# State sums for two tiles at a time, convolution taps loaded per image, and two edits at the first scan, in a four-layer convolutional block

## The chip, the cores and the metric

The kernel runs on one core of a Trainium2 chip. A core has five engines, each with its own instruction queue: TensorE (PE; matmuls, with its weight loads listed as PEld), VectorE (DVE), ScalarE (ACT), GpSimd (POOL) and SyncE (SP), which here issues nearly all DMA transfers. Within an engine instructions run in order; between engines they wait for one another by semaphores. Matmuls write to PSUM, which has eight banks of 128 x 512 float32; everything else lives in SBUF, 128 partitions wide, or in DRAM. The metric is the device time of one execution in microseconds.

## What is computed

The input x is 4 images of 128 channels and 64 x 64 pixels in float32. Four layers follow, each of the form x + layer(group norm of x), with 32 groups. Cut to what matters:

```python
# layer 0: attention over the 4096 pixels of an image (q, k, v from 128x128 matrices)
x = x + attention(gn(x))
# layer 1: 5x5 convolution whose 25 taps are built from radial tables
x = x + conv5(gn(x), build_kernel(weightsxx, weightsidentity, ...))
# layer 2: state space layer, channels 0-63 forward and 64-127 backward in the pixels
t  = Wx @ gn(x)
xc = silu(causal_conv4(t))                     # per direction, 64 channels
delta = softplus(Wd @ xc);  B = WB @ xc;  C = WC @ xc
h[l] = exp(delta * A) * h[l-1] + delta * xc * B   # 64 states per channel
y  = sum_over_states(h * C) + D * xc
x = x + Wp @ y
# layer 3: 3x3 convolution (its offset branch does not change the result)
x = x + conv3(gn(x), main_w) + main_b
```

For one image and one direction the state is 64 channels x 64 states, and the recurrence runs over 4096 pixels.

## The kernel before

**The scan and its ticks.** The recurrence of layer 2 is done by `scan_core` (L1160) as 1024 ticks of 128 rows x 1024 pixels. The ticks of an image (256 of them) run over four chunks of pixels, two directions d, 16 groups q of four states, and two halves g of 32 channels: a tile's 128 rows are 32 channels x 4 states. A tick i consists of steps that are issued at different distances, so that engines overlap: `load` four ticks ahead (SP fetches delta and delta*x, `de` and `dx`, spread over the states, when q is 0, and the B and C rows, `br` and `cr`, spread over the channels, when g is 0), `drive` two ahead (GpSimd, db = dx * br, L1228), `decay` one ahead (ScalarE, two exponentials of 512 pixels into PSUM banks, L1221), `recur` (VectorE, the scan itself, L1238, and for three ticks in five the product with C, L1241), `weigh` one behind (GpSimd, the product with C for the others, L1259) and `collect` three behind (TensorE). `collect` (L1261) does nothing for g = 0. For g = 1 it multiplies the two finished state tiles hc with a 128 x 32 selection matrix `sel` that sums over four states: four matmuls, one for each combination of half chunk and channel half, each into its own 32 partitions of one bank y (L1273). The bank gathers all 16 groups q; then the skip term D * xc is added (L1284), ScalarE copies the bank out, and SP stores it. State tiles hc come from a pool of six buffers (L1500).

**Work beside the scan.** All else is one long Python generator, `images` (L1450), and the main loop (L1518) draws from it. Each piece of work says what it costs TensorE in estimated microseconds; per tick 2.8 of such units are drawn (1.5 in the last image). So the order of instructions of every engine is fixed when the program is built. While image b is scanned, image b+1 goes through its front: its load and norm (`start`, `attention_start`), attention, the 5x5 convolution (`conv_pairs`) and the operands of its own scan (`scan_operands`). While image 3 is scanned, the ends of images 0 to 2 are done: output projection and 3x3 convolution. Image 0's own front runs alone at the beginning, and image 3's end alone at the end.

**Attention** (L434) walks through 256 steps u per image: a block of scores of 128 x 512 (L479), its exponential by ScalarE into a ring of eight 512-wide slots (L485), and the product with v two steps later (L491). The ring lies in a tile named `exchange`, which later holds delta. For image 0 the softmax sums are gathered by VectorE and GpSimd; for the others every four steps a group of four 32-column matmuls (`sums`, L507, tile zp) adds four ring slots. `sums_due` holds such a group back for up to a few steps, until a `collect` has just been issued (the flag "collected").

**The 5x5 convolution** works on pairs of rows. Its weights are the 25 taps, the sums of two pairs of tap rows (SUM12, SUM34), and for image 0 two further combinations (`more`). `build_conv_weights` (L231) makes taps and sums once, during image 0's attention, in a constant tile `cw` of 35 matrices of 128 x 128; `more_weights` makes the combinations in a pool `fill` that lives only until image 0's convolution is done. The first 15 matrices of `cw` are overwritten for the last layer (`m3`, LSUM, LDIF) when the last convolution is done, so they are also stored to DRAM (`kept`), from where a second, safe run of the program would get them back. That second run is taken only where softmax sums leave a range.

**Operands of the scan** (`scan_operands`, L998): per 512 pixels tap products (tile pt, `taps`), half of them into xc and their tanh (`halves`, L1030), the silu from both (`silu`, L1043), three products of xc (delta, B, C), softplus in several ScalarE steps, and stores to DRAM, from where the scan's rows are fetched. For image 0 the tanh goes to an SBUF buffer of the pool tag "w" (four buffers, shared with the B and C rows on their way out); for the others it stays in the bank pt.

**The load of image 1** (`start`, L1358, called beside image 0's operands with after = 10): it waits until image 0's operands no longer read the buffer (the flag "read"), lets ten turns pass, loads four pieces of 512 KB, lets ten more pass, and then takes the norm's statistics.

Of the kernel before, what the change touches and what calls it, by code (L numbers as in the profile page):

```python
# [24 lines left out]
F32 = mybir.dt.float32  # L25
# [7 lines left out]
P = 128  # L33
# [19 lines left out]
def conv_preact_kernel(  # L53
# [166 lines left out]


    SUM12, SUM34, HSUM, HDIF = 5, 6, 7, 8
    cw = const.tile([P, NTAP + 10, C], F32, name="cw")
    taps5 = cw[:, :NTAP, :]

    m3 = cw[:, : main_w.shape[1], :]

    LSUM, LDIF, NKEPT = 9, 12, 15
    kept = dram.tile([P, NKEPT, C], F32, tag="kept", bufs=1, name="kept")

    def build_conv_weights(tmp):  # L231
        xx_sb = tmp.tile([P, NTAP, C], F32, name="xx_sb")
        nc.sync.dma_start(xx_sb, xhat)
        id_sb = tmp.tile([P, C], F32, name="id_sb")
        nc.sync.dma_start(id_sb, identity)
        picked = tmp.tile([P, 2, NTAP, C // 2], F32, name="picked")
        for n, (which, table, inds) in enumerate((("xx", wxx, indsxx), ("id", wid, indsid))):
            nr, oc = table.shape[1], table.shape[2]
            acc = picked[:, n]
            one = cw.rearrange("p k c -> p (k c)")[:, : NTAP * oc]  # L240
            one = one.rearrange("p (k o) -> p k o", o=oc)
            tab = tmp.tile([P, nr, oc], F32, name=f"tab{which}")
            nc.sync.dma_start(tab, table)
            ii = tmp.tile([P, NTAP], I32, name=f"ii{which}")
            nc.sync.dma_start(ii, inds.to_broadcast([P, NTAP]))
            fi = tmp.tile([P, NTAP], F32, name=f"fi{which}")
            nc.vector.tensor_copy(fi, ii)

            ng = tmp.tile([P, NTAP], F32, name=f"ng{which}")
            nc.vector.tensor_scalar(ng, fi, 0.0, float(nr), ALU.is_lt, ALU.mult)  # L250
            nc.vector.tensor_tensor(fi, fi, ng, ALU.add)
            nc.vector.tensor_scalar(fi, fi, 0.0, float(nr - 1), ALU.max, ALU.min)
            for r in range(nr):
                hit = tmp.tile([P, NTAP], F32, name=f"hit{which}{r}")
                nc.vector.tensor_scalar(hit, fi, float(r), None, ALU.is_equal)
                hit_b = hit.unsqueeze(2).to_broadcast([P, NTAP, oc])
                tab_b = tab[:, r : r + 1, :].to_broadcast([P, NTAP, oc])
                if r == 0:
                    nc.vector.tensor_tensor(acc, tab_b, hit_b, ALU.mult)
                else:  # L260
                    nc.vector.tensor_tensor(one, tab_b, hit_b, ALU.mult)
                    nc.vector.tensor_tensor(acc, acc, one, ALU.add)
                yield HOP

        for t in range(2):
            def every(ap):
                return ap.rearrange("p k (o t) -> p k o t", t=2)[:, :NTAP, :, t]

            idb = id_sb.rearrange("p (o t) -> p o t", t=2)[:, :, t].unsqueeze(1)
            idb = idb.to_broadcast([P, NTAP, C // 2])  # L270
            nc.vector.tensor_tensor(every(xx_sb), every(xx_sb), picked[:, 0], ALU.mult)
            nc.vector.tensor_tensor(every(cw), picked[:, 1], idb, ALU.mult)
            yield HOP
        nc.vector.tensor_tensor(taps5, taps5, xx_sb, ALU.add)
        for n in range(2):
            row = cw[:, (1 + 2 * n) * 5 :]
            nc.vector.tensor_tensor(
                cw[:, NTAP + n * 5 : NTAP + (n + 1) * 5, :], row[:, :5], row[:, 5:10], ALU.add
            )
        nc.sync.dma_start(kept, cw[:, :NKEPT, :])  # L280

# [152 lines left out]
    def attention(b, xs, xn, v, st, safe, loads):  # L434
# [264 lines left out]


    def last_weights():
        half, above = cw[:, LSUM : LSUM + 3, :], cw[:, LDIF : LDIF + 3, :]
        nc.vector.tensor_tensor(half, m3[:, 0:3, :], m3[:, 6:9, :], ALU.add)
        nc.vector.tensor_scalar(half, half, 0.5, None, ALU.mult)
        nc.vector.scalar_tensor_tensor(above, m3[:, 3:6, :], -0.5, half, ALU.mult, ALU.add)
        nc.vector.scalar_tensor_tensor(half, m3[:, 3:6, :], 0.5, half, ALU.mult, ALU.add)

    def conv_last(b, xs, st, finish):
# [8 lines left out]
        def flat(t):  # L717
            return t.rearrange("p (h w) -> p h w", w=W)
# [30 lines left out]
        def products(acc, view, w):  # L749

            for n, dx in enumerate((1, 0, 2)):
                to = slice(max(1 - dx, 0), W - max(dx - 1, 0))
                of_ = slice(max(dx - 1, 0), W - max(1 - dx, 0))
                nc.tensor.matmul(  # L754
                    flat(acc)[:, :, to], cw[:, w + dx, :], view[:, :, of_],
                    start=n == 0, stop=n == 2, skip_group_check=True,
                )

# [36 lines left out]

    def more_weights(to):
# [12 lines left out]
    def conv_pairs(b, xs, tag, st, st2, lean):  # L811
# [99 lines left out]
        for c in range(L // CH):  # L911
# [20 lines left out]
            for n, (acc, parts) in enumerate(accs):  # L932
                k, total = 0, len(parts) * K5
                for w, view, r in parts:
                    for dx in range(K5):
                        k += 1
                        nc.tensor.matmul(  # L937
                            flat(acc), cw[:, w * K5 + dx, :] if w < HSUM else more[:, w - HSUM, dx, :],
                            view(r, dx), start=k == 1, stop=k == total and (n == 0 or not lean),
                        )  # L940
# [57 lines left out]
    def scan_operands(b, xn, mats4, piece):  # L998
# [31 lines left out]
        def halves(i):  # L1030
# [129 lines left out]
    def scan_core(mats4, ynds, before, widen, result):  # L1160
# [100 lines left out]
        def collect(i):  # L1261
# [2 lines left out]
            b, c, d, q, g = ticks[i]  # L1264
            if g + 1 < KG:
                return
            if q == 0:
                yacc[0] = bank("y", f"y_{b}_{c}_{d}")
            y = yacc[0]
            for h in range(CH // MM):  # L1270
                for gg in range(KG):
                    r = h * HALF + gg * SG
                    nc.tensor.matmul(  # L1273
                        y[r : r + SG, :], sel, hcs[i - KG + 1 + gg][:, bass.ts(h, MM)],
                        start=q == 0, stop=False, tile_position=(0, r), skip_group_check=True,
                    )
            ready.add("collected")
            for gg in range(KG):
                del hcs[i - KG + 1 + gg]
            if q + 1 < NQ:  # L1280
                return
            for h in range(CH // MM):
# [62 lines left out]
    def program(safe):  # L1345
# [2 lines left out]
        ready.clear()  # L1348
        shared.clear()
        if safe:  # L1350
            nc.sync.dma_start(cw[:, :NKEPT, :], kept)

        def load(tile, b):
            for c in range(NCH):
# [109 lines left out]
        with ExitStack() as es, tc.manual_schedule():  # L1464
# [19 lines left out]
            if not safe:  # L1484
                with tc.tile_pool(name="fill", bufs=2) as pools["fill"]:
                    while not (0, "begun") in ready:
                        next(work)
                    more = pools["fill"].tile([P, 2, 5, C], F32, tag="more", bufs=1, name="more")

                    with tc.tile_pool(name="tables", bufs=1) as tmp:  # L1490
                        for _ in chain(scan_constants(), build_conv_weights(tmp), more_weights(more)):
# [117 lines left out]
```

## Time and profile before

| what | value |
|---|---|
| median of three runs | 4463.48 us (4461.15 to 4466.09) |
| profiled run, and the span of its profile | 4455.06 us, 4453.2 us |
| TensorE busy in the span | 3977.4 us, 89% |
| VectorE busy | 3725.2 us, 84% |
| GpSimd busy | 3638.9 us, 82% |
| ScalarE busy | 2399.5 us, 54% |
| first and last drive (db) of scan 0 | 682 and 1635 us |
| of scan 1 | 1640 and 2583 us |
| of scan 2 | 2586 and 3529 us |
| of scan 3 | 3537 and 4375 us |
| scores of images 0, 1, 2, 3 | from 28, 731, 1676, 2620 us |

The span is the time from the first to the last instruction of the profiled execution; what lies around it makes the difference of 2 us to that run's time. A busy share over the whole span mixes stages with different limits. It must be read by stage, for which the drives give the borders: one tick has one drive, 256 ticks are a scan. The groups of the page that bear on the change (line, engine, operation, out<-in, count; then busy time, mean ns of one, and idle time before it with what ended most of it):

```profile
L1273 PE MATMUL y<-hc,sel 128*32 128x512 f32 x4096 | 652.1, 650 | 272.9 <-POOL hc L1259 264.6
L513 PE MATMUL zp<-exchange,ones 128*32 128x512 f32 x1536 | 201.6, 596 | 7.9 <-DVE xs L580 7.9
L1228 POOL TENSOR_TENSOR db<-dx,br 128x1024 f32<-128x1024 f32 x1024 | 2400.1, 2366 | 223.0 <-DMA dx<-dxd 53.1
```

A float32 matmul appears as two passes, so 4096 stands for 2048 matmuls in 512 calls of `collect`. Four of them run side by side in the array, hence 652 us busy at 650 ns each. The 265 us in which TensorE waits for a state tile lie almost wholly in scan 3, where TensorE has little to do.

### The profile page before, as it was taken

The page shows a single profiled execution, that of the slowest core. Times are in us where ns is not written, and L with a number is a line of the kernel's source. Part 1 is how long each engine was busy: PE and PEld are TensorE (multiplying, and loading weights), DVE is VectorE, ACT ScalarE, POOL GpSimd, SP SyncE. Part 2 cuts the span into 40 slices and gives each one's busy share as a digit, 9 for nine tenths or more (in the row PEclk, how much of TensorE's full clock was granted, in tenths as well). Part 3 has the DMA queues.
Part 4 walks back from the last instruction along what each step waited for, and adds up shares of the span by engine and source line. Part 5 has one row for each costly group of instructions (what it writes and reads, how often), then busy time and mean ns, then how long its engine had stood idle before and what let it go on. Part 6 is the DMA issues. An engine that isn't in the chain of part 4 may idle for free. (4 is left out here: it accounts for less than half of the span.)

```text
span 4453.2 us, 43584 instructions
## 1 busy us (share of the span) xinstructions
PE 3977.4 (89%) x13480; PEld 1470.5 (33%) x13480; DVE 3725.2 (84%) x3703; ACT 2399.5 (54%) x4425; POOL 3638.9 (82%) x1728
## 2 busy tenths in 40 slices
PE   8999998999999979999999989999999658576776
PEld 4444433333333323333333333333333112121222
DVE  4721218999999989999999899999999899999995
ACT  3333226666665476666664576666654754444532
POOL 3433307999999978999999889999999889999995
PEclk9999999999999989999999989999999878787888
DMA  1000016545554565454545565454545656656562
GB/s 63 9 1 1 0 59 229 177 169 175 177 175 157 178 231 196 173 174 172 182 158 175 200 227 175 172 181 170 177 160 177 224 213 210 226 197 231 188 227 79
DMA packets 210002, 719.86 MB, mean 162 GB/s; under 512 B 24800, under 2 KB 25696, under 8 KB 209632
## 3 DMA queue, kind: packets, MB, share of 16 engines
q1 hardware_dynamic: 208160, 716.26, 45.9%
q8 instruction: 108, 1.77, 0.2%
q14 instruction: 134, 1.10, 0.1%
q10 hardware_dynamic: 1600, 0.73, 0.1%
HBM read 649.07 MB, written 67.83 MB: 161 GB/s over the span
## 5 line engine op out<-in xcount | busy, mean ns | idle before, releaser
L1228 POOL TENSOR_TENSOR db<-dx,br 128x1024 f32<-128x1024 f32 x1024 | 2400.1, 2366 | 223.0 <-DMA dx<-dxd 53.1
L1221 ACT ACTIVATE da<-de,a_neg 128x512 f32<-128x512 f32 (+1 forms) x1796 | 1343.4, 751 | 683.3 <-DVE da L1238 393.7
L479 PE MATMUL sc<-r,x 128*128 128x512 f32 x2048 | 1085.2, 612 | 4.3 <-ACT r L448 3.2
L491 PE MATMUL acc<-exchange,v 128*128 128x512 f32 x2048 | 1047.7, 593 | 1.6
L1259 POOL TENSOR_TENSOR hc<-hc,cr 128x1024 f32<-128x1024 f32 x401 | 948.3, 2365 | 19.0 <-ACT last L1254 15.6
L485 ACT ACTIVATE exchange<-sc 128x512 f32<-128x512 f32 x1024 | 604.5, 590 | 577.4 <-PE sc L479 570.6
L1273 PE MATMUL y<-hc,sel 128*32 128x512 f32 x4096 | 652.1, 650 | 272.9 <-POOL hc L1259 264.6
L1241 DVE TENSOR_TENSOR hc<-da,cr 128x512 f32<-128x512 f32 (+1 forms) x1078 | 835.2, 775 | 69.8 <-issue 0.9
L1238 DVE TENSOR_TENSOR_SCAN da<-da,last,db 128x512 f32<-128x512 f32 (+1 forms) x464 | 728.0, 1569 | 15.3 <-POOL db L1228 13.4
L1238 DVE TENSOR_TENSOR_SCAN da<-da,da,db 128x512 f32<-128x512 f32 x455 | 585.5, 1287 | 21.1 <-ACT da L1221 20.4
L479 PEld LDWEIGHTS sc<-r,x 128*128 128x128 f32 x2048 | 360.5, 190 | 596.4 <-issue 387.1
L491 PEld LDWEIGHTS acc<-exchange,v 128*128 128x128 f32 x2048 | 386.9, 190 | 496.6 <-issue 478.3
L1238 DVE TENSOR_TENSOR_SCAN hc<-da,last,db 128x512 f32<-128x512 f32 (+1 forms) x304 | 455.6, 1499 | 3.7 <-POOL db L1228 2.0
L1238 DVE TENSOR_TENSOR_SCAN hc<-da,hc,db 128x512 f32<-128x512 f32 x317 | 406.7, 1283 | 40.9 <-ACT da L1221 10.7
L533 POOL TENSOR_TENSOR sidep<-sidep,exchange 128x512 f32<-128x512 f32 x120 | 170.7, 1423 | 273.4 <-ACT exchange L485 271.2
L1273 PEld LDWEIGHTS y<-hc,sel 128*32 128x32 f32 x4096 | 92.5, 111 | 727.0 <-POOL hc L1259 350.7
L533 DVE TENSOR_TENSOR sided<-sided,exchange 128x512 f32<-128x512 f32 x120 | 95.9, 799 | 221.5 <-ACT exchange L485 220.1
L937 PE MATMUL pe<-df,cw 128*128 128x512 f32 x560 | 253.3, 597 | 0.0
L1238 DVE TENSOR_TENSOR_SCAN da<-da,db 128x512 f32<-128x512 f32 (+1 forms) x159 | 236.0, 1484 | 10.4 <-ACT da L1221 7.2
L679 PE MATMUL pcm<-xpm,cw 128*128 128x512 f32 x432 | 227.8, 672 | 15.1 <-ACT xpm L384 15.1
L513 PE MATMUL zp<-exchange,ones 128*32 128x512 f32 x1536 | 201.6, 596 | 7.9 <-DVE xs L580 7.9
L1254 ACT COPY last<-da 128x1 f32<-128x1 f32 x474 | 73.9, 156 | 249.9 <-DVE hc L1241 247.9
(239 smaller groups left out, 2830.5 us busy)
## 6 DMA issues: line engine op xcount, KB each, us to landing
br<-bm SPq DMA_DIRECT2D x512, 512.0 KB, 5.2
cr<-cm SPq DMA_DIRECT2D x512, 512.0 KB, 3.9
de<-dd SPq DMA_DIRECT2D x64, 512.0 KB, 4.7
dx<-dxd SPq DMA_DIRECT2D x64, 512.0 KB, 6.1
x<-in_x_dram SPq DMA_DIRECT2D x16, 512.0 KB, 5.2
xs<-in_x_dram SPq DMA_DIRECT2D x16, 512.0 KB, 6.0
xsd<-xs SPq DMA_DIRECT2D x16, 512.0 KB, 6.8
xcd<-xc SPq DMA_DIRECT2D x16, 512.0 KB, 2.6
```

The costliest lines, as they stand in the source:

```text
L479: nc.tensor.matmul(sc, xn[:, bass.ts(j, P)], rq[blk], start=True, stop=True)
L485: nc.scalar.activation(pt, sc, AF.Exp)
L491: nc.tensor.matmul(acc[blk], v[:, j, :], ring[:, u % NRING, :], start=j == 0, stop=j == NJT - 1)
L533: eng.tensor_tensor(s, s, ring[:, u % NRING, :], ALU.add)
L679: nc.tensor.matmul(acc.rearrange("p (r w) -> p r w", w=W), weights[:, t, :], xp[:, y : y + RPM, dx : dx + W], start=t == 0, stop=t == k * ...
L937: nc.tensor.matmul(flat(acc), cw[:, w * K5 + dx, :] if w < HSUM else more[:, w - HSUM, dx, :], view(r, dx), start=k == 1, stop=k == total ...
L1221: nc.scalar.activation(da, rep["de", b, c, d, g][:, bass.ts(h, size)], AF.Exp, scale=a_neg[:, at(i)])
L1228: nc.gpsimd.tensor_tensor(dbs[i], rep["dx", b, c, d, g], rows["b", b, c, d, q], ALU.mult)
L1238: nc.vector.tensor_tensor_scan(h, da, db[:, cut], before, ALU.mult, ALU.add)
L1241: nc.vector.tensor_tensor(hc[:, cut], h, rows["c", b, c, d, q][:, cut], ALU.mult)
L1259: nc.gpsimd.tensor_tensor(hcs[i], hcs[i], rows["c", b, c, d, q], ALU.mult)
L1273: nc.tensor.matmul(y[r : r + SG, :], sel, hcs[i - KG + 1 + gg][:, bass.ts(h, MM)], start=q == 0, stop=False, tile_position=(0, r), skip_gr ...
```

## The change

State sums: `collect` acts on every second group q, and then sums both groups with eight matmuls, the older group first, in place of four matmuls for each group. Only the last two groups of the very last bank are still summed singly. The pool of state tiles grows from six to eight buffers.

```diff
-            if q == 0:
+            single = (b, c, d) == (B - 1, NCH - 1, 1) and q >= NQ - 2
+            if q % 2 == 0 and not single:
+                return
+            if q < 2:
                 yacc[0] = bank("y", f"y_{b}_{c}_{d}")
             y = yacc[0]
-            for h in range(CH // MM):
+            for back in range(0 if single else 1, -1, -1):
+                first = i - back * KG - KG + 1
+                for h in range(CH // MM):
+                    for gg in range(KG):
+                        r = h * HALF + gg * SG
+                        nc.tensor.matmul(
+                            y[r : r + SG, :], sel, hcs[first + gg][:, bass.ts(h, MM)],
+                            start=q == back, stop=False, tile_position=(0, r), skip_group_check=True,
+                        )
                 for gg in range(KG):
-                    r = h * HALF + gg * SG
...
+                    del hcs[first + gg]
             ready.add("collected")
...
-            pools["hc"] = es.enter_context(tc.tile_pool(name=f"hc{safe}", bufs=6))
+            pools["hc"] = es.enter_context(tc.tile_pool(name=f"hc{safe}", bufs=8))
```

Taps: the constant tile shrinks to 15 matrices (`cs`: the ten sums, later the last layer's weights). The 25 taps are built in the pool `fill` for image 0, stored to DRAM, and loaded for each later image into the ring of attention, slot by slot, as its last steps leave the slots; the convolution then reads them from there.

```diff
-    cw = const.tile([P, NTAP + 10, C], F32, name="cw")
+    cs = const.tile([P, 15, C], F32, name="cs")
+    m3 = cs[:, : main_w.shape[1], :]
+    kept = dram.tile([P, NTAP, C], F32, tag="kept", bufs=1, name="kept")
+    kept_sums = dram.tile([P, 10, C], F32, tag="kept_s", bufs=1, name="kept_sums")
...
+        def taps_to(n):
+            k = MM // C
+            to = ring[:, n, :].rearrange("p (k c) -> p k c", c=C)
+            part = kept[:, n * k : min((n + 1) * k, NTAP), :]
+            if not fill and part.shape[1]:
+                nc.sync.dma_start(to[:, : part.shape[1], :], part)
         values(N - 4)
         yield PRODUCT
         while due:
             sums(due.pop(0)[0])
             yield PRODUCT
+        for n in range(NRING - 4):
+            taps_to(n)
         if not fill:
             sums(N - 1)
             yield PRODUCT
+        taps_to(NRING - 4)
         evict_sums(blk)
         values(N - 3)
+        taps_to(NRING - 3)
         yield PRODUCT
         turn(blk)
         values(N - 2)
+        taps_to(NRING - 2)
...
+        taps5 = more[0] if wide else exchange(b)[:, : NTAP * C].rearrange("p (k c) -> p k c", c=C)
+        def matrix(w, dx):
+            if w < SUM12:
+                return taps5[:, w * K5 + dx, :]
+            if w < HSUM:
+                return cs[:, (w - SUM12) * K5 + dx, :]
+            return more[1][:, w - HSUM, dx, :]
```

The first scan: the load of image 1 also waits until the first chunk of image 0's operands is ready, and image 0's tanh is written over its own bank, as the other images' is.

```diff
+            while b == 1 and (0, "operands", 0) not in ready:
+                yield 0.0
             xn = large(b, f"x_{b}")[:, :L]
             yield from load(xn, b)
...
-            ths[i] = pt if b > 0 else pools["bg"].tile(
-                [P, MM], F32, tag="w", bufs=4, name=f"th_{b}_{i}"
-            )
+            ths[i] = pt
             nc.scalar.activation(ths[i], pt, AF.Tanh, scale=0.5, bias=hbias)
```

More of the change, by code (lines that the diff above doesn't have):

```diff
@@ L222, in conv_preact_kernel, with build_conv_weights @@
     SUM12, SUM34, HSUM, HDIF = 5, 6, 7, 8
-    cw = const.tile([P, NTAP + 10, C], F32, name="cw")
[L224 to L231, printed above, removed]
+    LSUM, LDIF = 9, 12
+    cs = const.tile([P, 15, C], F32, name="cs")
+    m3 = cs[:, : main_w.shape[1], :]
+    kept = dram.tile([P, NTAP, C], F32, tag="kept", bufs=1, name="kept")
+    kept_sums = dram.tile([P, 10, C], F32, tag="kept_s", bufs=1, name="kept_sums")
+    def build_conv_weights(tmp, cw):
+        taps5 = cw
         xx_sb = tmp.tile([P, NTAP, C], F32, name="xx_sb")
@@ L277, in build_conv_weights @@
             nc.vector.tensor_tensor(
-                cw[:, NTAP + n * 5 : NTAP + (n + 1) * 5, :], row[:, :5], row[:, 5:10], ALU.add
+                cs[:, n * 5 : (n + 1) * 5, :], row[:, :5], row[:, 5:10], ALU.add
             )
-        nc.sync.dma_start(kept, cw[:, :NKEPT, :])
+        nc.sync.dma_start(kept, cw)
+        nc.sync.dma_start(kept_sums, cs[:, :10, :])
     ASIZE, VSIZE = HP * (W + PAD) + PAD, (H + 2) * (W + 2) + PAD
@@ L701, in last_weights @@
     def last_weights():
-        half, above = cw[:, LSUM : LSUM + 3, :], cw[:, LDIF : LDIF + 3, :]
+        half, above = cs[:, LSUM : LSUM + 3, :], cs[:, LDIF : LDIF + 3, :]
         nc.vector.tensor_tensor(half, m3[:, 0:3, :], m3[:, 6:9, :], ALU.add)
@@ L754, in products @@
                 nc.tensor.matmul(
-                    flat(acc)[:, :, to], cw[:, w + dx, :], view[:, :, of_],
+                    flat(acc)[:, :, to], cs[:, w + dx, :], view[:, :, of_],
                     start=n == 0, stop=n == 2, skip_group_check=True,
@@ L787, in conv_last, with more_weights @@
             yield HOP
-    def more_weights(to):
+    def more_weights(cw, to):
         w = [cw[:, n * 5 : (n + 1) * 5, :] for n in range(3)]
@@ L937, in conv_pairs @@
                         nc.tensor.matmul(
-                            flat(acc), cw[:, w * K5 + dx, :] if w < HSUM else more[:, w - HSUM, dx, :],
-                            view(r, dx), start=k == 1, stop=k == total and (n == 0 or not lean),
+                            flat(acc), matrix(w, dx), view(r, dx),
+                            start=k == 1, stop=k == total and (n == 0 or not lean),
                         )
@@ L1266, in collect @@
                 return
-            if q == 0:
+            single = (b, c, d) == (B - 1, NCH - 1, 1) and q >= NQ - 2
+            if q % 2 == 0 and not single:
+                return
+            if q < 2:
                 yacc[0] = bank("y", f"y_{b}_{c}_{d}")
             y = yacc[0]
-            for h in range(CH // MM):
-                for gg in range(KG):
-                    r = h * HALF + gg * SG
[L1273 to L1276, printed above, removed]
+            for back in range(0 if single else 1, -1, -1):
[7 more added lines that the diff above has]
+                        )
+                for gg in range(KG):
+                    del hcs[first + gg]
             ready.add("collected")
-            for gg in range(KG):
-                del hcs[i - KG + 1 + gg]
             if q + 1 < NQ:
@@ L1350, in program @@
         if safe:
-            nc.sync.dma_start(cw[:, :NKEPT, :], kept)
+            nc.sync.dma_start(cs[:, :10, :], kept_sums)
         def load(tile, b):
@@ L1487, in program @@
                         next(work)
-                    more = pools["fill"].tile([P, 2, 5, C], F32, tag="more", bufs=1, name="more")
+                    more = [
+                        pools["fill"].tile([P, NTAP, C], F32, tag="taps", bufs=1, name="taps"),
+                        pools["fill"].tile([P, 2, 5, C], F32, tag="more", bufs=1, name="more"),
+                    ]
                     with tc.tile_pool(name="tables", bufs=1) as tmp:
-                        for _ in chain(scan_constants(), build_conv_weights(tmp), more_weights(more)):
+                        for _ in chain(scan_constants(), build_conv_weights(tmp, more[0]), more_weights(*more)):
                             for _ in range(4):
```

## The prediction

> **What bounds the kernel now.** I read the page's 40 slices first, then the sums of three stretches, then the waits in the longest of them, then TensorE's timeline across a few microseconds, and last the start of the first scan.
>
> ```profile
> PE   8999998999999979999999989999999658576776
> DVE  4721218999999989999999899999999899999995
> POOL 3433307999999978999999889999999889999995
> ```
>
> One digit is 111 us. Up to the sixth digit only TensorE is full: that is image 0's attention and 5x5 convolution. From the seventh to the 31st TensorE, VectorE and GpSimd are all full: scans 0 to 2, each with the front (attention, convolution, operands) of the next image. From the 32nd on TensorE has air: scan 3, with the ends of images 0 to 2. The sums (length; busy PE, PEld, DVE, ACT, POOL; clock; DMA) of an attention stretch, a convolution stretch and scan 3:
>
> ```profile
> 760.00:1300.00 540.00, 535.37 (x2046) 196.78 (x2045) 510.61 (x524) 348.54 (x719) 502.91 (x218) 1.00 0.51 176
> 1385.00:1562.00 177.00, 176.84 (x540) 65.73 (x541) 167.73 (x175) 81.43 (x129) 172.50 (x79) 0.99 0.49 166
> 3540.00:4380.00 840.00, 561.32 (x1662) 154.35 (x1662) 810.83 (x479) 393.99 (x624) 798.94 (x361) 0.79 0.60 212
> ```
>
> Beside attention TensorE has 4.6 us left of 540, VectorE 29, GpSimd 37: TensorE sets the pace, by 5%. Beside the convolution TensorE has nothing left, GpSimd 4.5 of 177. In scan 3 TensorE is idle a third of the time and VectorE and GpSimd decide. The waits in the attention stretch (total us, times, longest):
>
> ```profile
> DVE da L1238 <- ACT da L1221: 4.8, 8, 1.6
> ACT exchange L485 <- PE sc L479: 71.0, 81, 2.5
> ACT da L1221 <- DVE da L1238: 62.6, 57, 3.5
> PE y L1273 <- POOL hc L1259: 1.3, 1, 1.3
> ```
>
> ScalarE waits for TensorE's scores and for VectorE's decay banks: it runs ahead of both. VectorE hardly waits for ScalarE. TensorE waits for a state tile 1.3 us in all, so the sums over the states (y) are never early there. Now what one such sum costs:
>
> ```profile
> 1361.85 1.02 PE L491 MATMUL acc<-exchange,v 128*128 128x512 f32 x2
> 1362.70 1.02 PE L479 MATMUL sc<-r,x 128*128 128x512 f32 x2
> 1363.66 1.06 PE L1273 MATMUL y<-hc,sel 128*32 128x512 f32 x8
> 1364.54 1.04 PE L513 MATMUL zp<-exchange,ones 128*32 128x512 f32 x8
> 1365.51 1.12 PE L479 MATMUL sc<-r,x 128*128 128x512 f32 x2
> 1366.47 1.02 PE L491 MATMUL acc<-exchange,v 128*128 128x512 f32 x2
> ...
> 1371.23 1.07 PE L1273 MATMUL y<-hc,sel 128*32 128x512 f32 x8
> 1372.22 1.13 PE L491 MATMUL acc<-exchange,v 128*128 128x512 f32 x2
> ```
>
> The reader compares starts, since the ends are modelled. A full product followed by another takes 0.86. A full product before a 32-column burst takes 0.95 (1362.70 to 1363.66), and one after a burst 0.96 (1365.51 to 1366.47). A burst between full products takes 0.99 (1371.23 to 1372.22); two bursts in a row take 0.88 and 0.97. Over the whole of 800 to 1300 us the medians of these gaps are 0.858, 0.952, 0.963, 0.996, 0.882 and 0.972, nearly without spread. So a lone burst costs 0.996 + 0.094 + 0.105 = 1.195 us, and one that joins another costs 0.882 + 0.972 - 0.996 = 0.858: **each join saves 0.337 us of TensorE.**
>
> **What the Trainium skill says.** "TensorEngine Tiling (Array Packing)", Tiling Modes, Key Properties: "Changing tiling mode (not just tile) drains the TensorE". The trace agrees, with the 0.337 us above as the price of going into the mode and out. "TensorE: Matmul & The Clock Gate", Part 3, has column tiles run side by side for about the time of one matmul. The trace agrees: four matmuls of 32 columns (eight passes) add 0.858, as long as one full product. "PSUM — Partial Sum Buffer", Specifications (TRN2), calls ScalarE "faster to PSUM than to SBUF": tanh takes 661 ns into its bank (images 1 to 3) and 687 into SBUF (image 0). "DMA: Bandwidth & Descriptors", Issuing engines are not separate DMA queues: transfers share 16 engines and interleave; so a moved load slows what is issued beside it.
>
> **The change part by part.**
>
> *State sums for two tiles.* The arithmetic stays: as many y matmuls. I counted the 32-column bursts in the order in which the two programs issue their matmuls. Beside attention (neighbours sc or acc) 320 become 253; beside the convolution 83 become 42; beside keys and operands 24 become 13; in scan 3 96 become 53. Attention gains less than half of its bursts, because a softmax sum (zp) now finds a y burst to join half as often: 43 lone zp bursts become 114. That gives 67 x 0.337 = 22.6 us, 41 x 0.337 = 13.8, 11 x 0.337 = 3.7, and 43 x 0.337 = 14.5. What of it reaches the end: beside attention TensorE leads by 5% and the saving is 1.2%, so I take 85%, 19 us. Beside the convolution 4.6 us per image meet GpSimd's 4.5 of air, so I take 60%, 8. At the borders (TensorE busy 145 of 165 us from 1575 to 1740) half, 2. In scan 3 nothing, since VectorE and GpSimd end there. Sum: **-29 us**, between -6 and -40. No wait is added: the last state tile of a burst is as old as before (three ticks), and with 8 buffers in place of 6 a tile is written again two ticks after its sum was issued, as before. The tail is kept single, so the last y is not later.
>
> *Image 1's load behind the scan's rows.* This moves image 1's norm behind other work. Before:
>
> ```profile
> 654.79 1.41 SPq L1355 DMA_DIRECT2D x<-in_x_dram  x3
> 688.38 0.91 POOL L378 TENSOR_TENSOR rs_a<-back_a,mhalf 128x1 f32<-128x1 f32 x1 [3.60 <-DVE back_a L376]
> 697.89 2.07 PE L411 MATMUL pv<-wv,x 128*128 128x128 f32 x8 [3.86 <-ACT x L384]
> 730.57 4.69 PE L479 MATMUL sc<-r,x 128*128 128x512 f32 x6 [0.84 <-ACT r L448]
> ```
>
> In the new order SP issues two of the four x loads just ahead of the first de, dx, br and cr rows and two just behind them; the second tick's de and dx come after these. At the 400 GB/s that broadcast rows reach here, 1 MB is 2.6 us, so the first two drives (db) start some 3 us late; both had slack (the first drive ended at 684.8, its scan began at 692.8). The norm's rs_a on GpSimd now stands behind four joins (5.0 us from 706.7), two products delta*x (4.7), a drive and a weighing (2.4 each), which start when ScalarE's logarithms end: 703.1 before, up to 6 us earlier now, since eight bn_stats (8 x 0.64) and the norm's 2.4 us leave VectorE's path to the last operands. So rs_a comes at 711 to 718. ScalarE then has four normalisations (4 x 1.14), eight v copies (8 x 0.53), two table loads and two logarithms (3.7), eight decays (8 x 0.65) and small copies: 18 us, then r. First scores at 730 to 738 against 730.6. The scores stand after the same tick in both programs and TensorE is full from there on, so the shift counts whole: **+4 us**, between -4 and +12.
>
> *Image 0's tanh in its bank.* It saves 26 ns on each of eight activations. The bank is held until the silu, some 1.5 us longer; its next user is delta's product of two tiles later or a tap product behind it, both of which need or follow that silu. 0.
>
> *Taps per image.* Three times seven DMAs of up to 256 KB from DRAM into the freed ring, 1.6 MB per image. At 176 GB/s and a share of 0.51 there is room: 9 us of transfer, where the first tap of the ring is read no earlier than the last sc (1366) plus norm (to 1385) plus the q products from the constant tile (ten products, 9 us). SP must wait for TensorE to have read a ring slot before it issues; queued behind are the br and cr rows of four ticks ahead (14 us at 3.5 us a tick, landing in 4 to 5). **+1 us**, between 0 and +6. The weights' DVE work for image 0 is the same.
>
> Sum: -29 + 4 + 1 = -24. The profiled span is 4453.2, its run 4455.06; so 4429 and 4431. The median of the runs lies 8.4 above that run: **4463.5 - 24 = 4440 us**. The ends: -40 - 4 + 0 gives 4419, -6 + 12 + 6 gives 4475.
>
> **The rivals.** *Hidden anyway*: VectorE needs 3.8 us for a tick that it weighs itself and 2.5 for one that GpSimd weighs, 3.3 in the 3-to-2 mix, plus the front's own work, of 3.5 measured; if small stalls between the three full engines eat the join's gain, a fifth of it is left, 8 us, less 5: 4460. For it: the 5% of VectorE's air is bursts of queueing, not a reserve. Against: its waits add to 11 us in 540.
>
> *Slower*: a double y burst holds the score stream for 0.86 us more, and with a zp for 2.9 us in all. ScalarE is in order: exp of a score (L485) waits, and the decays (L1221) queued behind it reach VectorE's scan (L1238) late. In images 0 to 2 there are 192 double bursts, 192 x 0.86 = 165 us; from 15% of it (24 us) the gain is gone, and at a third the kernel is 55 - 24 = 31 us slower: 4494. For it: ScalarE already waits 71 us for scores. Against: three decay banks, and 63 us in which ScalarE waits for VectorE to free one.
>
> *The start*: if image 1's norm waits not 30 but 75 us, because its loads and GpSimd's joins line up, the whole front is 45 us later instead of 4: 4480. It decides from 28 us on. Against: TensorE's own list of keys is only 20 us long. *More than forecast*: all 40 us arrive and TensorE's shorter waits let the ends of images finish sooner in scan 3: 4418.
>
> That the change doesn't do what it says holds for one part: half of image 1's load is still issued ahead of the first rows. It is in the sum.
>
> **How the numbers follow.** Forecast 0.62 (its own range 4422 to 4454), more 0.06, hidden 0.14, slower by the decays 0.12, by the start 0.06. A measurement of this kernel tells 0.2%, 9 us, from no change. Faster: 0.62 + 0.06 = 0.68; same: 0.14; slower: 0.18. The range 4415 to 4475 leaves out most of the two slower cases and the end of the gain.
>
> **What would show it.** Right: about 160 fewer switches into 32-column mode, y groups of x16 at 1.85 us; 16 ticks in attention go from 56 to about 55 us; TensorE still at 98% or more there; first scores between 727 and 740; scan 3 as long as before (838 us from its first drive to its last). Wrong: VectorE's waits for ScalarE's da grown from 8 us to over 30 in the same stretch; POOL or DVE waiting for DMA br after the taps; a TensorE gap at pe ahead of the convolution; a join worth less than 0.3 us.

## The result: 7.7 us faster, a third of the forecast

| | before | after |
|---|---|---|
| median of twelve runs each | 4459.02 us (4454.52 to 4466.09) | 4451.28 us (4447.34 to 4456.33) |
| ratio after / before | | 0.9981 [0.9973, 0.9989] |
| profiled run, span | 4455.06, 4453.2 us | 4449.49, 4447.7 us |

The changed kernel is faster by 7.7 us (5 to 12 by the interval). The forecast was 24 less. The time lies inside the stated range of 4415 to 4475, and the sign is right. But the size is that of the rival "hidden anyway" (8 us left of the joins). The median of three runs from which the forecast was counted was itself 4.5 us high: twelve runs give 4459.0.

The slices of the changed kernel's page, one digit for 111 us:

```profile
PE   8999997999999979999999889999999657575666
DVE  4722217999999989999999899999999899999995
POOL 3433307999999978999999889999999889999995
```

They tell nearly nothing: no stage has gone from full to free. The sums by stretch tell more (length; busy PE, PEld, DVE, ACT, POOL; clock; DMA share, GB/s), for attention, convolution and scan 3:

```profile
760.00:1300.00 540.00, 533.64 (x2060) 199.41 (x2059) 513.00 (x527) 349.75 (x721) 503.45 (x217) 1.00 0.51 177
1385.00:1562.00 177.00, 175.21 (x551) 68.86 (x552) 168.55 (x176) 82.32 (x129) 173.81 (x82) 0.98 0.48 166
3540.00:4370.00 830.00, 524.38 (x1644) 155.34 (x1648) 800.59 (x472) 386.11 (x614) 790.15 (x359) 0.78 0.60 212
```

In the attention stretch TensorE issues 2060 passes in place of 2046 and still shows 99% busy. VectorE's 524 instructions have become 527, in the same 540 us. So this stage moves through its work only half a per cent faster. The groups of the page for the two kinds of 32-column bursts (busy us, mean ns | idle before):

```profile
L1302 PE MATMUL y<-hc,sel 128*32 128x512 f32 x4096 | 596.2, 641 | 267.2 <-POOL hc L1282 254.4
L516 PE MATMUL zp<-exchange,ones 128*32 128x512 f32 x1536 | 203.9, 600 | 12.0 <-DVE xs L583 12.0
```

The same 4096 passes of y are busy 596.2 us; they were busy 652.1. Over the whole span TensorE's busy time fell from 3977.4 to 3911.7, by 66 us, while the span fell by 5.5. Half of the 66 lies in scan 3 (557.46 before, from 3540 to 4370 us), where TensorE is idle a third of the time. **The work has gone; the time has not gone with it.** TensorE's timeline shows the joins in place (start, duration, then the group):

```profile
908.65 1.02 PE L494 MATMUL acc<-exchange,v 128*128 128x512 f32 x2
910.08 1.06 PE L516 MATMUL zp<-exchange,ones 128*32 128x512 f32 x8 [0.41 <-DVE xs L583]
911.08 1.12 PE L482 MATMUL sc<-r,x 128*128 128x512 f32 x2
912.04 1.02 PE L494 MATMUL acc<-exchange,v 128*128 128x512 f32 x2
912.99 1.92 PE L1302 MATMUL y<-hc,sel 128*32 128x512 f32 x16
914.84 1.13 PE L482 MATMUL sc<-r,x 128*128 128x512 f32 x2
```

From start to start: a double y burst between full products takes 1.85 (912.99 to 914.84), a lone zp 1.00 (910.08 to 911.08). The medians over 800 to 1300 us are 1.854 for the double and 0.996 for the lone one, so the second burst costs 0.858, as priced.

To see where time went I took the starts of the 1024 drives (db) and summed by stage (us). I divided the 256 ticks of a scan into 16 at its start, 160 beside attention, 16 after them, 48 beside the convolution and 16 at the border; "48 other ticks" are the three groups of 16:

| stage | before, scans 0 / 1 / 2 | after | change in all |
|---|---|---|---|
| to the first drive | 682.4 | 684.8 | +2.3 |
| 160 ticks, attention | 558.6 / 560.6 / 560.3 | 557.9 / 557.6 / 557.5 | -6.5 |
| 48 ticks, convolution | 176.9 / 165.7 / 167.3 | 175.1 / 165.8 / 166.1 | -2.9 |
| 48 other ticks | 221.8 / 219.4 / 224.3 | 223.2 / 218.3 / 224.1 | 0 |
| scan 3 | 838.1 | 838.9 | +0.8 |

A row repeats to 1 to 3 us between profiles of like kernels (experiment 1 against the kernel before: +3.0 in the attention row, +1.0 in the convolution row), so only attention stands clear of that. Attention itself runs from about tick 8 to tick 191, so the 160 ticks are its inner part. By the traces of the two kernels the groups of adjoining 32-column bursts fall there from 276 to 223. That is 53 of attention's 67 joins, and at 0.337 us each it is 17.9 us. In the 48 convolution ticks they fall from 71 to 36: 35 joins, 11.8 us. Of these sums, 6.5 and 2.9 us arrived.

### The profile page after: what moved, and what is told of

It is laid out like the page before. It is cut to its first block, busy times and chain, and to the rows that moved or that the text cites. A ratio compares the mean times of both kernels' runs of the same rounds, so it can differ in the third digit from the quotient of the medians.

```text
span 4447.7 us, 43619 instructions
## 1 busy us (share of the span) xinstructions
PE 3911.7 (88%) x13480; PEld 1490.8 (34%) x13480; DVE 3722.9 (84%) x3703; ACT 2397.9 (54%) x4425; POOL 3637.5 (82%) x1728
## 5 line engine op out<-in xcount | busy, mean ns | idle before, releaser
L1302 PE MATMUL y<-hc,sel 128*32 128x512 f32 x4096 | 596.2, 641 | 267.2 <-POOL hc L1282 254.4
L1261 DVE TENSOR_TENSOR_SCAN da<-da,last,db 128x512 f32<-128x512 f32 (+1 forms) x464 | 728.3, 1570 | 15.9 <-POOL db L1251 12.3
L1261 DVE TENSOR_TENSOR_SCAN da<-da,da,db 128x512 f32<-128x512 f32 x455 | 585.5, 1287 | 17.0 <-ACT da L1244 16.6
L1261 DVE TENSOR_TENSOR_SCAN hc<-da,last,db 128x512 f32<-128x512 f32 (+1 forms) x304 | 455.7, 1499 | 2.7 <-POOL db L1251 1.4
L1261 DVE TENSOR_TENSOR_SCAN hc<-da,hc,db 128x512 f32<-128x512 f32 x317 | 406.7, 1283 | 42.6 <-ACT da L1244 12.4
L1302 PEld LDWEIGHTS y<-hc,sel 128*32 128x32 f32 x4096 | 114.2, 112 | 687.6 <-POOL hc L1282 341.5
L1261 DVE TENSOR_TENSOR_SCAN da<-da,db 128x512 f32<-128x512 f32 (+1 forms) x159 | 236.0, 1484 | 10.1 <-ACT da L1244 7.7
L696 PE MATMUL pcm<-xpm,cs 128*128 128x512 f32 x432 | 213.7, 644 | 34.4 <-ACT xpm L387 34.4
L962 PE MATMUL pe<-df,exchange 128*128 128x512 f32 x480 | 213.7, 595 | 0.0
```

Of the source, the lines that this page charges most:

```text
L696: nc.tensor.matmul(acc.rearrange("p (r w) -> p r w", w=W), weights[:, t, :], xp[:, y : y + RPM, dx : dx + W], start=t == 0, stop=t == k * ...
L962: nc.tensor.matmul(flat(acc), matrix(w, dx), view(r, dx), start=k == 1, stop=k == total and (n == 0 or not lean),)
L1261: nc.vector.tensor_tensor_scan(h, da, db[:, cut], before, ALU.mult, ALU.add)
L1302: nc.tensor.matmul(y[r : r + SG, :], sel, hcs[first + gg][:, bass.ts(h, MM)], start=q == back, stop=False, tile_position=(0, r), skip_grou ...
```

## The experiments

Times are medians; ratios are to runs of the kernel before on the same chip, where its median was 4459.8 us in the first four, 4459.6 in the next four and 4462.0 in the last three.

**1. Is it the joins, and does another part take something back?** The changed kernel with the old `collect`; the eight state buffers, taps, start and tanh stay as changed.

```diff
-            for back in range(0 if single else 1, -1, -1):
-                first = i - back * KG - KG + 1
-                for h in range(CH // MM):
...
+            for h in range(CH // MM):
+                for gg in range(KG):
```

> The changed kernel with one part undone: the states of one group are summed at a time again (four matmuls every two ticks), all else as changed, the eight state buffers too. Theory V (VectorE sets the pace beside attention and convolution, the joined sums gave only 6 to 9 us): 4457 to 4461, about as the kernel before. Theory S (the joined sums gave the forecast 29 us, and another part of the change took 20 back): the other part alone is left, so 4475 to 4485.

Measured: 4459.85 us, ratio 0.9998 [0.9989, 1.0006]. The joins are worth the whole gain, about 8 us, and the other three parts together nothing (-5 to +3 by the interval). The theory that another part takes 20 us back falls. The +3.0 in its attention row lies all in scan 0 (+3.2; scans 1 and 2: +0.4 and -0.7), where the moved load acts. Whether that is a cost of the start or scatter, this run can't tell.

**2 and 3. Is VectorE a second wall?** An engine's wall is here the time that 160 ticks would take if that engine alone set it; to relieve an engine is to take work from it. The product of the state with C is left out in 144 of VectorE's ticks, once on the kernel before and once on the changed one, so both kernels leave a factor out of their output.

```diff
-                h = hc[:, cut] if to_pool(i) else da
+                bare = b + 1 < B and i % 5 == 2
+                h = hc[:, cut] if to_pool(i) or bare else da
...
-                if not to_pool(i):
+                if not to_pool(i) and not bare:
```

> The kernel before, with VectorE relieved: in one tick in five of images 0 to 2 (144 ticks) the product with C is left out and the scan writes the state tile itself; the output lacks that factor. It takes 144 x 2 x 0.61 = 175 us from VectorE and nothing from TensorE, and leaves the order of the work as it is. Theory V: VectorE is the first bound, but TensorE, with 4 to 5 us of idle time in 560, is the second right behind it, so 10 to 30 us faster than before, no more. Theory T (TensorE set the pace before): no more than 5 us faster.

> The changed kernel with VectorE relieved in the same way (the product with C left out in 144 ticks of images 0 to 2; the output lacks that factor). Theory V: with VectorE out of the way the shorter work of TensorE shows: 30 to 40 us less than the relieved kernel before (the joins' 22.6 + 13.8 us beside attention and convolution and a part of the borders' 3.7, less the 3 us of the start), where the plain kernels differ by 8. Theory S: the difference between the two relieved kernels stays near 8 us.

Measured: 4438.1 us, 0.9945 [0.9932, 0.9959], and 4414.24 us, 0.9895 [0.988, 0.991]. The second run is 21.7 us under the kernel before, as theory V expected, so VectorE bounded that kernel too; theory T, which allowed 5, falls. With VectorE's load as it is, the change is worth 8 us. With VectorE relieved, the same change is worth 23.9 (15 to 33 by the two intervals). The ticks say where: from the second run to the third, the 160 ticks lose 12.4 us in all and the convolution's 48 lose 9.4; between the plain kernels they lost 6.5 and 2.9. The direction is what theory V asked for; the 30 to 40 us that it expected were too much. That 23.9 comes close to the 24 of the forecast is chance: the forecast had 29 for the joins and took 5 off for the start and the taps.

The waits of the attention stretch show the load change sides (us in total, times, longest; da and hc of L1261 are both outputs of VectorE's scan). The changed kernel:

```profile
ACT da L1244 <- DVE da L1261: 63.3, 59, 2.4
ACT exchange L488 <- PE sc L482: 61.9, 71, 2.7
ACT da L1244 <- DVE hc L1261: 35.8, 56, 1.0
...
DVE da L1261 <- ACT da L1244: 2.9, 3, 1.8
```

The third kernel, VectorE relieved:

```profile
ACT exchange L488 <- PE sc L482: 121.9, 123, 3.4
ACT da L1244 <- DVE da L1262: 24.6, 25, 1.9
ACT da L1244 <- DVE hc L1262: 12.2, 23, 1.0
...
DVE hc L1262 <- ACT da L1244: 23.9, 23, 3.1
DVE da L1262 <- ACT da L1244: 12.7, 16, 3.4
```

ScalarE feeds both engines. In the changed kernel it waits for both: 99 us for VectorE's scan (63.3 + 35.8) and 62 for TensorE's scores. With VectorE relieved, ScalarE waits 37 us for VectorE and twice as long as before for TensorE, and VectorE itself now waits 37 us for ScalarE.

**4. The same from TensorE's side.** The changed kernel, with only the last of every eight softmax-sum groups of a block; the output lacks the others.

```diff
-            if j == 3:
+            if j < NJT - 1:
+                return
+            if j == NJT - 1:
...
-                    ring[:, (u - 3 + g) % NRING, :], start=j == 3, stop=j == NJT - 1,
+                    ring[:, (u - 3 + g) % NRING, :], start=True, stop=j == NJT - 1,
```

> The changed kernel with TensorE relieved still more: of the eight groups of softmax sums of each block of images 1 to 3 only the last is computed, so the normaliser is that of four tiles in 32; the order and the estimated costs of the rest stay. It takes 168 bursts from TensorE, at 0.86 to 1.2 us each 144 to 200 us, and next to nothing from the other engines. Theory V: TensorE is no longer the bound, so 0 to 12 us less than the changed kernel. Theory T (TensorE still sets the pace): 100 us less or more.

Measured: 4431.45 us, 0.9938 [0.9924, 0.9951]: 19.8 less than the changed kernel. That is some way over the 12 us that theory V allowed, and far under the 100 of theory T, in which TensorE alone sets the pace. In the attention stretch the waits are now:

```profile
ACT da L1246 <- DVE da L1263: 113.0, 79, 2.7
ACT da L1246 <- DVE hc L1263: 42.1, 61, 1.0
...
ACT exchange L488 <- PE sc L482: 10.6, 16, 1.6
...
DVE da L1263 <- ACT da L1246: 1.4, 2, 1.0
```

ScalarE hardly waits for scores and almost only for VectorE. VectorE's waits of all kinds come to 2 to 6 us in the 160 ticks: it is full, with 160 ticks in 551 us. TensorE stands idle for 34 to 40 us of them.

**5. Both relieved.** The edits of 3 and 4 together, on the changed kernel.

> The changed kernel with both reliefs of the two runs before together: the product with C left out in 144 ticks of images 0 to 2, and of the softmax sums of images 1 to 3 only the last group of each block; the output lacks both. Each relief alone stopped after 20 to 37 us. Theory V (two walls of nearly the same height, VectorE's and TensorE's, and nothing else between 550 and 530 us per 160 ticks): the next wall is GpSimd, which is busy some 518 us of them, so 4340 to 4390. Rival Q (a common cause stops both, such as ScalarE's order of exponentials or the waits from engine to engine): no lower than 4400.

Measured: 4332.53 us, 0.9716 [0.9701, 0.9731]. That is 119 us under the changed kernel. The two reliefs alone took 37 and 20, so half of the effect, 62 us, needs both at once. It is 7 us more than the most that theory V expected. Rival Q, that a common cause and neither engine is the limit, falls, since it allowed nothing under 4400. A stretch of this kernel (columns as above):

```profile
1750.00:2250.00 500.00, 478.45 (x1619) 186.38 (x1617) 467.30 (x469) 334.53 (x695) 492.15 (x217) 0.99 0.53 185
```

The next wall is probably GpSimd, 492 of 500 us busy, at 527 us for 160 ticks: there it is idle for 7 to 9 us, TensorE for 11 to 13, and VectorE waits for 17 to 19. No run relieves GpSimd, so this rests on the trace alone. Lined up, 160 ticks in us, mean of scans 0 to 2:

| kernel | 160 ticks | which engine sets the time |
|---|---|---|
| before | 559.8 | TensorE and VectorE |
| before, VectorE relieved | 555.5 | TensorE |
| after | 557.7 | TensorE and VectorE |
| after, VectorE relieved | 551.3 | TensorE |
| after, TensorE relieved | 551.0 | VectorE |
| after, both relieved | 527.4 | GpSimd, by the trace |

TensorE's wall fell by 4.2 and met VectorE's, 551.3 against 551.0. (VectorE's wall before is taken to be the same 551.0, since its work is the same.) With both in place the kernel stands 6.5 above either, where before it stood 4.3 above the higher one. So half of the 4.2 is spent on the two engines holding each other up. These means repeat to about 1 us (560.8 in experiment 1 against 559.8), so this share is rough.

**6 to 8. Can GpSimd take work from VectorE?** It is idle for about 36 us in 160 ticks. So 35 (or 18) of VectorE's products with C go to GpSimd, on the changed kernel and, the same 35, on the kernel before.

```diff
-                    else n % 2 == 0 if "operands" in ready else n % 2 == 1
+                    else n % 2 == 0 if "operands" in ready else n % 2 == 1 or i % 20 == 0
```

> The changed kernel with a complete result, in which GpSimd takes 35 more products with C of images 0 to 2 from VectorE (every twentieth tick in the usual pattern). VectorE loses 35 x 1.22 = 43 us, GpSimd gains 35 x 2.36 = 83 us. Theory V: VectorE's wall falls below TensorE's (550 us per 160 ticks), and the joins show as far as GpSimd's air reaches: 5 to 12 us less than the changed kernel, 4440 to 4446. Rival Q: no change or slower, since GpSimd is the third of three full engines: 4450 to 4465.

> As the run before, with half as many: 18 more products with C go to GpSimd (every fortieth tick). Theory V: 3 to 7 us less than the changed kernel. Rival Q: within 3 us of it.

> The kernel before, with the same 35 products more for GpSimd, and a complete result. Theory V: TensorE's wall stands at 554 to 557 us per 160 ticks here, of 560, so 2 to 10 us less than before, and the changed kernel with the same edit is 8 to 20 us below this one. Rival Q: no change or slower.

Measured: with 35 moved 4453.96 us, 0.9984 [0.9977, 0.9991]; with 18 (`i % 40` in the diff) 4451.51, 0.9983 [0.9975, 0.9991]; on the kernel before 4466.5, 1.0019 [1.0013, 1.0026]. Moving work gains nothing on the changed kernel and loses 7 us on the other. The gains that theory V expected in all three runs did not come; rival Q had these three right. VectorE's waits in 1750 to 2250 us show where the relief went. The changed kernel:

```profile
DVE da L1261 <- ACT da L1244: 4.1, 3, 2.7
DVE hc L1261 <- ACT da L1244: 2.8, 6, 1.0
```

With 35 products moved:

```profile
DVE da L1261 <- ACT da L1244: 6.9, 5, 2.9
DVE hc L1261 <- ACT da L1244: 6.8, 10, 1.5
DVE da L1261 <- POOL db L1251: 4.7, 8, 1.3
```

VectorE has 11 us less to do in this stretch (465.11 us busy in place of 476.52) and spends what it saves on waiting: 18 us for ScalarE and for GpSimd's drives, in place of 7. GpSimd still has 17 to 21 us of 160 ticks unused. The joins are worth 12.5 us between the sixth and the eighth kernel, inside the 8 to 20 of theory V; by the intervals that isn't clear of the 7.7 between the plain kernels.

**9 to 11. Do the fronts want to be drawn faster?** The units of front work drawn per tick rise from 2.8 to 2.86 or 2.92, since TensorE's real work per unit has shrunk.

```diff
-PRODUCT, HOP, SLOT, PACE, ENDPACE, AHEAD = 0.86, 1.7, 0.7, 2.8, 1.5, 4
+PRODUCT, HOP, SLOT, PACE, ENDPACE, AHEAD = 0.86, 1.7, 0.7, 2.86, 1.5, 4
```

> The changed kernel with the share of front work per tick raised from 2.8 to 2.86 estimated us (2%), result complete. The joins have made TensorE's wall in attention 4 us per 160 ticks lower; this gives the room back to it: per tick 2% more front work, so the front is done some 5 ticks earlier and less of it is left for the border between two scans, where TensorE and VectorE both idle. Theory V: the stretch beside attention becomes 2 to 6 us longer per image, the border 5 to 12 us shorter, net 3 to 15 us less than the changed kernel. Rival: the borders are bound by the chain of image b+1's operands and do not shorten, so 5 to 15 us more than the changed kernel.

> As the run before with 2.92 (4% more). Theory V: TensorE's wall rises over VectorE's, so no better than 2.86 and perhaps worse than 2.8. Rival: 10 to 30 us more than the changed kernel.

> The kernel before with 2.86. Theory V: TensorE's wall is already the higher one here, so each per cent more front work in a tick costs its whole time beside attention; within 5 us of before or slower, and 8 to 20 us above the changed kernel with 2.86.

Measured: on the changed kernel 2.86 gives 4468.17 us, 1.0014 [1.0007, 1.0021], and 2.92 gives 4499.14, 1.0088 [1.0074, 1.0102]; 2.86 on the kernel before gives 4482.75, 1.0046 [1.0032, 1.006]. At 2.86 the expected gain of 3 to 15 us is a loss of about 15 to 17 from the changed kernel, just over the rival's 5 to 15. At 2.92 the loss is 48, which theory V left room for and the rival's 10 to 30 did not. On the kernel before it is about 21, also as theory V had it. In the ninth kernel the 160 ticks of attention are 9, 7 and 14 us longer. Since one unit more per tick also moves every stage to other ticks, what each later stage gives back can't be separated. What is shown is that the pace of 2.8 isn't too low for the shorter bursts. Whether it is too high stays open: a kernel with 2.76 was meant to show it, but there is no time of it. The joins are worth 14.6 us at 2.86 (about 8 to 22 by the intervals).

No version in this study beats the changed kernel with the same output. The joins alone, on the old taps, were not tried: their two buffers take 8 KB of each partition, and the smaller constant tile (20 matrices of 512 bytes per partition less) frees 10 KB. So "the taps are worth nothing" is a statement on their time alone.

## Why the prediction was right in sign and wrong in size

- **A join saves 0.337 us of TensorE: right.** The double burst measures 1.854 where 0.996 + 0.858 was reckoned. The Trainium skill's "TensorEngine Tiling (Array Packing)", Key Properties, on which it leaned (a change of mode drains the engine), agrees in this trace too, with 1.854 us for two bursts in a row where two lone ones take 1.992. The counts were right as well: the traces have 523 groups of bursts before and 361 after, 162 fewer, as in 67 + 41 + 11 + 43.
- **"TensorE sets the pace, by 5%", and so 85% of attention's 22.6 us arrive: this is the step that failed.** In the 160 ticks 6.5 of 17.9 us arrived, 36%; over attention as a whole, from the first score to the last product with v, 9.8 of 22.6 (1925.3 us for three images before, 1915.5 after), 43%. The 5% was read from shares: VectorE "29 us left of 540" against TensorE's 4.6. But VectorE's idle time is not all air, that is, time in which it could do more. In 160 ticks of the kernel before it is idle for 29 to 30 us, of which 18 to 20 are gaps of under 0.2 us between one instruction and the next, and only 10 to 11 are waits. So VectorE's wall stands near 560 - 11 = 549 us, and relieving TensorE confirmed it at 551. TensorE's own stood at 555.5: a lead of under 1%, less than the saving that it was to let through. The forecast had this as its rival and argued against it with the very number, "its waits add to 11 us in 540". Those 11 us were the whole margin.
- **"Beside the convolution 60%", 8 us: 2.9 arrived.** The forecast set its limit by GpSimd's 4.5 us of air. VectorE had hardly more: of its 8 to 13 us idle in the 48 ticks before, 3.4 to 7.0 are waits. With VectorE relieved the same joins bring 9.4 of the 11.8 us that lie in these ticks.
- **Borders 2, scan 3 nothing: right within the scatter** (all ticks of scans 0 to 2 outside attention and convolution 0, scan 3 +0.8). In scan 3 43 of the joins fall into idle time of TensorE, as forecast.
- **The start, "the shift counts whole": wrong, on the other side.** The rows beside the moved load landed some 2 us later, as reckoned (the first dx 6.2 us after its issue in place of 4.6, the second 8.5 in place of 6.6). The norm's step on GpSimd came at 715.5, as forecast (711 to 718):

```profile
715.48 0.55 POOL L381 TENSOR_TENSOR rs_a<-back_a,mhalf 128x1 f32<-128x1 f32 x1 [1.51 <-DVE back_a L379]
```

The first scores start at 738.8, 8 us later than before and just above the 730 to 738 given. But the ticks hardly moved: measured from the first tap product of image 0's operands, 16 ticks are over after 122.6 us in the changed kernel and after 121.5 in the one before. By the first experiment start, taps and tanh together cost 0 (at most 3) and not 5. So a later first score did not reach the end whole, though TensorE is full from there on; that VectorE's wall hides it is likely, but no run tests it.
- **The taps: +1 of 0 to 6, right** as far as the first experiment tells (the three parts together 0). GpSimd's waits for `br` from 690 to 3500 us are 14.8 us in all, in place of 19.6; TensorE's wait at the convolution's first product is 7.6, 9.0 and 8.7 us for images 1 to 3, in place of 7.6, 8.0 and 7.7.
- **Rivals.** "Hidden anyway" was right that VectorE's air was no reserve and in its 8 us for the joins, and should have had the larger chance. The size is luck in part, since its "fifth" of the gain had no working, and with 5 us for the start it put the time at 4460, not 4451. "Slower by the decays" is refuted: VectorE's waits for `da` did not grow (4.8 us before, 2.9 after), and ScalarE's for scores fell from 71.0 to 61.9. A longer burst that held the score stream would have raised both. (The "63 us" of this rival were only part of the reading: with the waits for hc, 31.2 us, ScalarE waited 94 us for VectorE's scan in the kernel before.)

The total is nearer than its parts: the joins were put 21 us too high, and the 5 us for start and taps, which did not come, took some of that back. That the time falls into the stated range is no proof of the mechanism: no change at all would have lain inside it too.

What stays open: with VectorE relieved, the 160 ticks got 12.4 us of the 17.9 that the joins free there. A row repeats to 1 to 3 us, so a part of the other 5.5 may be scatter; which engine keeps the rest wasn't settled.

## What to carry to other kernels

Before pricing what a faster engine brings, find the height of the next wall: split that engine's idle time into waits and the short gaps between its instructions, and take only the waits as air. Here that gives 549 us from the profile of before, and the run with TensorE relieved gave 551. Where two engines come within a per cent or two of each other, run each relieved of some work, and both: two walls show as a relief of both that is worth far more than the two alone (here 119 us against 37 + 20). The waits of an engine between the two do not settle it by themselves. ScalarE waited 94 us for VectorE and 71 for TensorE before, but also 92 and 52 with both relieved, where the trace points to neither of them.

## What the runs showed that was not expected

A TensorE row that is 99% full did not prove that TensorE alone sets the pace. In 1750 to 2250 us it is busy 496.58 us before and 494.61 after, though by the joins in them 160 ticks bring it 1.1% less work (17.9 us in three times 560). The Trainium skill says of matmul busy time that it "is not a good measure of how close you are to roofline" ("Perfetto Trace Analysis", Identifying the Most-Contended Engine), and the trace agrees. I added up by how much each group of matmuls takes longer to the next start than is usual for its kind between the same neighbours (the 10th percentile). That gives 8 us in 160 ticks before, 10 to 12 after, and 51 to 55 with TensorE relieved. The profile shows part of this as idle time (3 to 4, 5 to 7 and 34 to 40 us); the rest, about 4, 5 and 16 us, is inside "busy". The same section takes the busy share of VectorE as a fair measure; here 95% busy was already the wall, for the 16 to 20 us of short gaps did not close in any of the runs.

GpSimd's 7% of idle time could not be used by moving products to it (experiments 6 to 8): the time that VectorE saved became waits. It isn't beyond use as such, since with both other engines relieved only 7 to 9 us of it are left. Why the moved products found no use for it stays open.
